# Two attention layers on one core: next input and left operands of layer 1 in pieces of 8 KB a partition

## The chip, the cores and the metric

The kernel runs on one core of a Trainium2 chip. The core has a matrix engine (TensorE, PE in the profile; its weight loads are PEld), a vector engine (DVE), a scalar engine (ACT), a general one (GpSimd, POOL) and SyncE (SP), which issues most of the DMAs here. The DMAs of all queues run on 16 DMA engines. The metric is the device time of one execution in microseconds (us); smaller is better.

## The reference, cut to what matters

The input is x of shape (8, 512, 32, 32), float32: eight batches of 512 channels by 1024 tokens. Two layers follow one another, each with a residual and a group norm ahead of it:

```
x = x + L0(gn(x))        # qkv projection, 8-head attention, output projection
x = x + L1(gn(x))        # below

q, k, v = w_q @ x, w_k @ x, w_v @ x                    # 512x512 each, 8 heads of 64
attn = einsum('bhdq,bhdT->bhqT', q, k) * scale
attn = softmax(einsum('gh,bhqT->bgqT', w_head, attn))  # heads mixed before the softmax
attn = instance_norm(attn) * gamma + beta
out  = einsum('bhqT,bhdT->bhqd', attn, v).reshape(b, t, c) @ w_proj.T + b_proj
```

## The kernel before, in words

Layer 0 runs for all eight batches, then layer 1 for all eight. Between them the result of layer 0 lies in DRAM: `x1_d[b]`, 512 x 1024 float32, one row a channel (L503). Layer 0 writes it in eight tiles of 128 x 512 a batch (L1080). Layer 1 reads it twice: as the input `y` (L1270 for batch 0, `y_piece`, L1372, for the others) and again for the residual (L1564, `xs`, and L1620, `xs_last`, for the last batch).

The projections with `w_k`, `w_q` and `w_proj` are done by a Strassen-like scheme with seven products. Its left operands are seven combinations of blocks of the weights, fields 0 to 6 of 2 KB a partition each. Layer 0 makes them once (L792) and keeps them in DRAM as `left_d`, one row of 14 KB a partition; layer 1 loads them again for each batch. `Projection.products` (L1406) says which field a product uses, and `ORDER` (L1396) in which order the products come.

**The steps of layer 1.** Attention of a batch b goes in steps p = 0 to 8, each of four parts t = 0 to 3 (`Attention1.step`, L1930). In a step p from 2 to 7:

- PE computes the scores of 128 queries: eight tiles `scores(p, 0..7)` (L1701), which ACT copies out of PSUM to `raw` (L1713). `raw` has two buffers: one for tiles 0 to 3, the first half (kh = 0), one for tiles 4 to 7, the second half (kh = 1).
- SP then regroups `raw` by DMAs from SBUF to SBUF: `regroup` (L1719), per half eight DMAs of 256 KB, s = 0 to 3 with two each, so 16 in a step. They are issued for the first half in parts 1 and 2, for the second half at the end of the step. They put the heads of one query group on the partitions, for the mixing of heads.
- `mix(p - 1, s)` (L1738) mixes the heads of the step before on PE; it needs the regrouped quarter s of both halves. `mix(p - 1, 0)` comes 4.75 us after the first scores of step p when nothing is late: three scores tiles and half a `values` (L1796) lie before it. `mix` takes two PSUM tiles out of three, the ones that the scores tiles leave when ACT has copied them.
- ACT takes the exponentials (L1751), DVE transposes them (L1766) and takes their statistics (L1780), PE multiplies with v (L1796).
- In odd steps (3, 5, 7) the sums of two steps are turned into reciprocals: `totals` (L1828) has three more small matmuls, four small DMAs by POOL to DRAM (`zd`, L1844), and then two DMAs of 256 KB by POOL that broadcast them to all partitions (`rzb`, L1856). These two belong to the next step in the order of the code, but POOL gets to them when the `zd` have landed: in steps 3 and 5 of every batch, and in step 7 of the last one, within the same step.

**The pieces.** While batch b is in its steps, the data of batch b + 1 are loaded in pieces, one a step, issued by SP in part t = 0 of steps 2 to 7 (`piece`, L2008, from the list `a.pieces`, L2049): four pieces of `y` (a chunk of 128 channels each, 512 KB, 4 KB a partition), then fields 0-1 and fields 4-5 of `left_k` (512 KB each). Fields 2-3 and field 6 follow in step 8. SP takes its instructions in the order of the code: in step p a piece stands behind the second half of the regroups of step p - 1 and ahead of the first half of step p. In the last batch there is no next one: the pieces are four chunks of `w_proj` of 256 KB, in steps 2 to 5 (L2072), and steps 6 and 7 have none.

SP's DMAs share eight semaphores in turn; a DMA waits until the one eight places before it has landed.

What follows the steps (from the first scores of step 7 to the first scores of the next batch) takes 127.6 us in every batch; it holds the other projections, `out1`, and the loads of `left_p`, `left_q` and `w_v`.

Of the kernel before, what the change touches and what calls it, by code (L numbers as in the profile page):

```python
# [9 lines left out]
F32 = mybir.dt.float32  # L10
# [8 lines left out]
P = 128  # L19
# [448 lines left out]
def tile_two_attention_layers(  # L468
# [19 lines left out]
    nc = tc.nc  # L488
# [11 lines left out]

    const = ctx.enter_context(tc.tile_pool(name="const", bufs=1))
    dram = ctx.enter_context(tc.tile_pool(name="dram", bufs=1, space=DRAM))
    x1_d = [dram.tile([C, T], F32, tag=f"x1_{b}", name=f"x1_{b}") for b in range(B)]  # L503


    def column(name, src):
# [206 lines left out]
    with ExitStack() as l0:  # L713
# [35 lines left out]
        }  # L749
        left_t = {}  # L750

        def left_tile(which, b):
            t = wpool.tile([P, 7, 2, HC], F32, tag="left", name=f"left_{which}_{b}")
            left_t[which] = t
            return t

        def load_left(which, b):
            t = left_tile(which, b)
            nc.sync.dma_start(out=t.rearrange("p f k o -> p (f k o)"), in_=left_d[which])

        a21 = {}

# [18 lines left out]
        def combine_left(which, parts=range(5)):  # L781
            t, a = left_t[which], a21[which]
            if 0 in parts:
                nc.vector.tensor_add(t[:, 3], a, t[:, 2])
            if 1 in parts:
                nc.vector.tensor_sub(t[:, 4], t[:, 3], t[:, 0])
            if 2 in parts:
                nc.vector.tensor_sub(t[:, 5], t[:, 0], a)
            if 3 in parts:
                nc.vector.tensor_sub(t[:, 6], t[:, 1], t[:, 4])  # L790
            if 4 in parts:
                nc.sync.dma_start(out=left_d[which], in_=t.rearrange("p f k o -> p (f k o)"))  # L792

        load_blocks("k")
        load_blocks("v")
# [266 lines left out]
        def out0(b):  # L1062
            def finish(i, j, x, y):
                if y is not None and isinstance(x, list):
                    for m in range(2):
                        nc.vector.tensor_add(y[:, m], y[:, m], x[m])
                    x = y
                elif y is not None:

                    into = x if j == 1 and i == 1 else y  # L1070
                    nc.vector.tensor_add(into, y, x)
                    x = into
                for m in range(2):
                    oc = 2 * i + m
                    dst = xs[b][oc][:, ts(j, FB)]
                    xm = x[m] if isinstance(x, list) else x[:, m]
                    nc.vector.scalar_tensor_tensor(
                        dst, xm, pb0[:, oc : oc + 1], dst, ALU.add, ALU.add
                    )
                    nc.sync.dma_start(out=x1_d[b][ts(oc, P), ts(j, FB)], in_=dst)  # L1080

            project0(f"pp0_{b}", "p", xa_t[b], finish)

# [158 lines left out]
        for b in range(B):  # L1242
            more = b + 1 < B
            ag = Agenda()
            ag.at(1, lambda: bias_xa(b))
            for c in range(NCC):
                ag.at(2 + 2 * c, lambda c=c: start_xa(b, c))
            for c, slot in enumerate((4, 7, 12, 15)):
                if b > 0:
                    ag.at(slot, lambda c=c: stats_out(b - 1, c))  # L1250
                if more:
                    ag.at(slot + 1, lambda c=c: load_x(b + 1, c))
            if b < 3:

                which = ("k1", "q1", "p1")[b]
                ag.at(1, lambda which=which: load_blocks(which, tag="junk"))
                for i, slot in enumerate((13, 14, 16, 17, 19)):
                    ag.at(slot, lambda which=which, i=i: combine_left(which, [i]))
            if more:
                stats0(b + 1, ag, 18)  # L1260
                for c in range(NCC):
                    ag.at(51 + 3 * c, lambda c=c: normalize0(b + 1, c))
                ag.at(32, lambda: load_left("k", b + 1))
                ag.at(33, lambda: load_left("v", b + 1))
            else:

                def load_first():
                    t = n_t["1"] = shared.tile([P, NCC, T], F32, tag="n", name="y_0")
                    for c in range(NCC):
                        nc.sync.dma_start(out=t[:, c], in_=x1_d[0][ts(c, P), :])  # L1270

                ag.at(20, load_first)
                for slot, fn in zip((22, 25, 28), group_stages(0, B - 1, small_psum)):
                    ag.at(slot, fn)
                ag.at(32, lambda: load_left("q1", 0))
                ag.at(33, lambda: load_left("k1", 0))
                for c in range(NCC):
                    ag.at(49 + 4 * c, lambda c=c: normalize_to(n_t["1"][:, c], 0, c))
            attention0(b, ag)
            slot = NI + 2  # L1280
            if more:
                combine_right(f"{b + 1}", n_t[b + 1])
                qk0(b + 1, "k")
            else:
                combine_right("y1", n_t["1"])
                first_q1()
            ag.flush()
            if more:
                load_left("q", b + 1)
                v0(b + 1)  # L1290
                load_left("p", b)
                qk0(b + 1, "q")
            else:
                load_left("p", b)
                first_k1()
                first_wv()
            combine_right(f"{b}_xa", xa_t[b])
            out0(b)
            tmp.clear()
# [6 lines left out]
    with ExitStack() as l1:  # L1306
# [58 lines left out]
        def p_piece(c):  # L1365

            if c == 0:
                left_tile(("p", B - 1))
                w_t["p", B - 1] = w_t["p", B - 1][:, :NCC]
            nc.sync.dma_start(out=w_t["p", B - 1][:, c], in_=w_projT[ts(c, P)])  # L1370

        def y_piece(b, c):  # L1372

            if c == 0:
                y_t[b] = shared.tile([P, NCC, T], F32, tag="n", name=f"y_{b}")
            nc.sync.dma_start(out=y_t[b][:, c], in_=x1_d[b][ts(c, P), :])

        def normalize1(b, c):
            normalize_to(y_t[b][:, c], b, c)
# [15 lines left out]
        class Projection:  # L1395
# [10 lines left out]
            def products(self, m):  # L1406
                w = w_t[self.key]
                left, right = {
                    1: (0, self.b11), 2: (1, self.b21), 3: (6, self.b22), 4: (2, self.t[:, 3]),
                    5: (3, self.t[:, 0]), 6: (4, self.t[:, 1]), 7: (5, self.t[:, 2]),  # L1410
                }[m]
                if m == 2:
                    self.ps[2] = self.ps.pop(1)
                else:
                    self.ps[m] = m_psum(f"{self.nm}_{m}")
                for i in range(2):
                    for k in range(2):
                        nc.tensor.matmul(
                            self.ps[m][:, i], w[:, left, k * HC + i * P : k * HC + i * P + P],
                            right[:, k], start=(k == 0 and m != 2), stop=(k == 1),  # L1420
                            skip_group_check=True,
                        )
# [135 lines left out]
        def out1(b, t):  # L1558
# [4 lines left out]
            for i, j in ((0, 0), (1, 1), (1, 0), (0, 1)):  # L1563
                nc.sync.dma_start(  # L1564
                    out=xs[i][:, :, ts(j, FB)],
                    in_=x1_d[b][i * 2 * P : (i + 1) * 2 * P, ts(j, FB)].rearrange(
                        "(m p) t -> p m t", p=P
                    ),
                )

            def begin(i, j, y):
# [21 lines left out]
        def out1_last(a):  # L1593
# [22 lines left out]
            def inputs():  # L1616

                x = rawpool.tile([P, NCC, T], F32, tag="raw", name="xs_last")
                for oc in range(NCC):
                    nc.sync.dma_start(out=x[:, oc], in_=x1_d[b][ts(oc, P), :])  # L1620
                wsum = epool.tile([P, 2 * T], F32, tag="e", name="wsum")[:, :C]
                nc.vector.tensor_add(wsum, w[:, 0], w[:, 1])
                for n in range(2, NCH):
                    nc.vector.tensor_add(wsum, wsum, w[:, n])
                kept.extend((x, wsum))
# [61 lines left out]
        class Attention1:  # L1687
# [242 lines left out]
            def step(self, p, t, ag):  # L1930
# [73 lines left out]
                        self.regroup(p, kh, s)  # L2004
                if t == 3 and p % 2 == 0 and p >= 4:
                    self.divide(p // 2 - 2, nc.gpsimd)
                if older and t == 0:
                    self.piece()  # L2008
                ag.run(4 * p + t)

# [22 lines left out]
        for b in range(B):  # L2033
# [12 lines left out]
                    ag.at(i, stages[i])  # L2046
                ag.at(3, v_sums)
            if more:
                a.pieces += [lambda c=c: y_piece(b + 1, c) for c in range(NCC)]  # L2049
                a.pieces += [lambda f=f: left_piece(("k", b + 1), f, 2) for f in (0, 4)]  # L2050
                ag.at(4 * NT, lambda: left_piece(("k", b + 1), 2, 2))
                ag.at(4 * NT, lambda: left_piece(("k", b + 1), 6, 1))
                for c in range(NCC):
                    ag.at(24 + c, lambda c=c: normalize1(b + 1, c))

# [13 lines left out]
                ag.at(4 * NT + 1.5, lambda: k_go(6))  # L2069
                ag.at(4 * NT + 2.5, lambda: k_go(7))  # L2070
            else:
                a.pieces += [lambda c=c: p_piece(c) for c in range(NCC)]  # L2072

                def prelude():
                    out_products.extend(out1_last(a))
# [108 lines left out]
```

## Time and profile before

| what | value |
|---|---|
| median of 3 runs | 3907.03 us (3902.49 to 3908.03) |
| profiled execution, its own time | 3899.99 us |
| its span, from the first to the last instruction | 3898.1 us |
| granted TensorE clock | 0.999 |
| DVE, ACT, POOL busy | 73%, 50%, 5% of the span |
| first scores of layer 1, batch 0, step 0 | at 1778.4 us |
| a batch of layer 1, from its step 0 to the next one's | 269.4 to 271.3 us (batches 1 to 6) |
| DMA issues on SP's queue | 1024 regroups, 28 `y` pieces, 28 pieces of `left_k`, others |

The page names, for each line of the kernel, the busy time of its group of instructions, and then the idle time of that engine just ahead of them and what ended it. Views of the waits, of the timeline and of chosen stretches of time (windows) go into a part of the span. Landings of single DMAs come from the trace's semaphore records: each DMA counts its semaphore up sixteen times, once for each DMA engine, and the last of these is its landing. Positions in a step are counted from its first scores matmul (L1701).

### The profile page before, as it was taken

What the parts mean: (1) busy time and instruction counts of PE and PEld (TensorE: products, weight loads), DVE (VectorE), ACT (ScalarE), POOL (GpSimd) and SP (SyncE); (2) the same over time, 40 slices, a digit from 0 to 9 for tenths busy, and PEclk for the clock granted to TensorE, in tenths of its full rate; (3) what the DMA queues carried; (4) which work ended last, traced back from release to release, by engine and by line L of the source; (5) the groups of instructions that cost most, each with busy time, mean ns of one, the idle gap of its engine ahead of it and who ended that gap; (6) DMA issues with size and microseconds to landing.
All of it is one profiled execution on the core that took longest, in us unless ns stands there. A gap on an engine that the chain in (4) does not pass through costs nothing. (4 is left out here: it accounts for less than half of the span.)

```text
span 3898.1 us, 95183 instructions
## 1 busy us (share of the span) xinstructions
PE 3845.0 (99%) x41612; PEld 1809.6 (46%) x41612; DVE 2840.8 (73%) x3921; ACT 1962.0 (50%) x2400; POOL 207.4 (5%) x210
## 2 busy tenths in 40 slices
PE   8999999999999999999999999999999999999999
PEld 4353535344353535344554544545545545445455
DVE  4858586675859485866967958859769668678598
ACT  1726354453627172534826717528438257176175
POOL 0000000000000000000110200201101102002000
PEclk9999999999999999999999999999999999999999
DMA  3313131111122121216947929749659479297385
GB/s 122 123 52 118 50 113 43 67 67 71 58 73 67 59 81 49 91 47 162 235 133 194 231 91 232 194 127 240 180 136 239 150 171 237 96 222 206 119 222 161
DMA packets 248440, 519.45 MB, mean 133 GB/s; under 512 B 49872, under 2 KB 57040, under 8 KB 241360
## 3 DMA queue, kind: packets, MB, share of 16 engines
q1 hardware_dynamic: 240832, 500.48, 45.3%
q0 software_dynamic: 7184, 12.81, 1.6%
q8 instruction: 328, 5.37, 0.6%
q14 instruction: 96, 0.79, 0.1%
HBM read 197.16 MB, written 46.92 MB: 63 GB/s over the span
## 5 line engine op out<-in xcount | busy, mean ns | idle before, releaser
L1766 DVE STREAM_TRANSPOSE et<-e 128x2048 f32<-128x2048 f32 x256 | 590.0, 2305 | 190.4 <-ACT e L1751 189.3
L1796 PEld LDWEIGHTS a<-et,v 128*64 128x64 f32 x16384 | 505.7, 138 | 283.8 <-issue 266.1
L1780 DVE BATCH_NORM_STATS2 bn<-e 128x6 f32<-128x512 f32 x1024 | 635.7, 683 | 0.0
L1107 ACT ACTIVATE e<-s 128x1024 f32<-128x1024 f32 x512 | 496.9, 1024 | 233.0 <-PE s L1102 233.0
L1713 ACT COPY raw<-s 128x1024 f32<-128x1024 f32 x480 | 470.1, 1018 | 224.8 <-PE s L1701 201.3
L1751 ACT ACTIVATE e<-m 128x1024 f32<-128x1024 f32 x512 | 496.2, 1021 | 165.7 <-issue 62.4
L1796 PE MATMUL a<-et,v 128*64 128x64 f32 x16384 | 553.3, 224 | 0.0
L1701 PE MATMUL s<-k,q 64*64 64x512 f32 x4096 | 513.2, 605 | 2.7 <-DVE v L1060 1.4
L1102 PE MATMUL s<-q,k 64*64 64x512 f32 x4096 | 490.4, 594 | 2.3 <-ACT e L1107 2.3
L1117 DVE TENSOR_TENSOR zacc<-zacc,e 128x1024 f32<-128x1024 f32 x384 | 467.5, 1217 | 27.2 <-ACT e L1107 1.4
L1130 PE MATMUL a<-e,v 64*64 64x512 f32 x4096 | 484.1, 589 | 0.0
L1738 PE MATMUL m<-re,wmix 32*32 32x512 f32 x8192 | 306.2, 599 | 14.8 <-DMA re<-raw 11.8
L1130 PEld LDWEIGHTS a<-e,v 64*64 64x64 f32 x4096 | 156.7, 133 | 282.8 <-issue 282.5
L1102 PEld LDWEIGHTS s<-q,k 64*64 64x64 f32 x4096 | 146.2, 133 | 284.4 <-issue 220.2
L1844 POOL DMA_DIRECT2D zd<-rz x96 | 52.5, 552 | 3361.9 <-DMA y<-x 1846.6
L1701 PEld LDWEIGHTS s<-k,q 64*64 64x64 f32 x4096 | 127.2, 132 | 216.0 <-issue 95.5
L1812 ACT COPY q<-a 64x256 f32<-64x256 f32 x256 | 94.0, 367 | 138.7 <-PE a L1796 137.1
L1738 PEld LDWEIGHTS m<-re,wmix 32*32 32x32 f32 x8192 | 68.1, 103 | 154.3 <-ACT raw L1713 65.9
L1509 PE MATMUL pv_t<-wv,y 128*128 128x512 f32 x256 | 120.6, 609 | 0.0
L920 PE MATMUL pv_p<-left_v,tmp 128*128 128x256 f32 x512 | 113.1, 379 | 0.0
L920 PE MATMUL pk_p<-tmp,left_k 128*128 128x512 f32 x256 | 112.5, 592 | 0.0
L920 PE MATMUL pq_p<-tmp,left_q 128*128 128x512 f32 x256 | 112.5, 592 | 0.0
(332 smaller groups left out, 3918.3 us busy)
## 6 DMA issues: line engine op xcount, KB each, us to landing
re<-raw SPq DMA_DIRECT2D x1024, 256.0 KB
left_q<-left_q SPq DMA_DIRECT2D x17, 1792.0 KB
left_p<-left_p SPq DMA_DIRECT2D x17, 1792.0 KB
left_k<-left_k SPq DMA_DIRECT2D x10, 1792.0 KB
x<-in_x_dram SPq DMA_DIRECT2D x32, 512.0 KB
rzb<-zd SPq DMA_DIRECT2D x128, 128.0 KB
x<-x SPq DMA_DIRECT2D x64, 256.0 KB
y<-x SPq DMA_DIRECT2D x32, 512.0 KB
```

The lines of the kernel that those rows point to most:

```text
L920: nc.tensor.matmul(out, st, mv, start=start, stop=(k == 1), skip_group_check=True)
L1102: nc.tensor.matmul(ps[c * D : c * D + D, m], k[r, hp, k0 : k0 + D], q[r, hp, ts(f, FB)], start=True, stop=True,)
L1107: nc.scalar.activation(e[i], ps, AF.Exp, scale=S0 * S0)
L1117: nc.vector.tensor_add(zacc[g], zacc[g], e[i])
L1130: nc.tensor.matmul(acc[g][a][m * D : m * D + D], v[rows, kc, ts(2 * hp + m, D)], e[i][rows, m], start=(kc == 0), stop=(kc == NG - 1),)
L1701: nc.tensor.matmul(ps[c * D : c * D + D, m], qo_t[b][r, p, hp, ts(c, D)], k_t[b][r, hp, ts(kh, FB)], start=True, stop=True,)
L1713: nc.scalar.copy(dst, ps)
L1738: nc.tensor.matmul(ps[a // 2][c * 32 : c * 32 + 32, a % 2].rearrange("p (r h k) -> p h r k", r=2, h=2), wmix[rows].rearrange("p g i -> p ( ...
L1751: nc.scalar.activation(e[:, :, 2 * h : 2 * h + 2].rearrange("p r a k -> p a r k"), ps[h].rearrange("p a (r k) -> p a r k", r=2), AF.Exp,)
L1766: nc.vector.transpose(self.et[p, u].rearrange("p kb (r st a) g q -> p st kb r (a g q)", r=2, st=2)[:, st], self.e[p, s].rearrange("p r a ( ...
L1780: nc.vector.bn_stats(self.bn[n][:, p % 2, s, a], e[:, :, a].rearrange("p r k -> p k r"))
L1796: nc.tensor.matmul(acc[two * D : two * D + D, s].rearrange("p (x q) -> p x q", q=4), v_t[b][:, kb, ts(g, D)], et[:, kb, :, g], start=(kb = ...
```

## The change

- `x1_d[b]` becomes 256 x 2048: row p of block i holds channel p of chunk 2i and then channel p of chunk 2i + 1, so that two chunks are 8 KB side by side for a partition. Layer 0's writes, the two loads of `y` and the residual's loads follow that layout.
- A `y` piece is two chunks: 1 MB, 8 KB a partition. There are two instead of four.
- In DRAM (for the three weights of layer 1) the fields lie in the order 0, 1, 4, 5, 2, 3, 6. The first piece of `left_k` is fields 0, 1, 4, 5 (1 MB, 8 KB a partition); the rest, fields 2, 3, 6 (768 KB), is one DMA in step 8. `products` has the new places of the fields.
- Layer 0 writes and reads these three left operands in four DMAs instead of one, since its own tiles keep the old order of fields.
- A piece is issued in steps 2, 4 and 6 alone, not in 2 to 7. The last batch loads two chunks of `w_proj` in step 2 and two in step 4.

```diff
-    x1_d = [dram.tile([C, T], F32, ...) for b in range(B)]
+    x1_d = [dram.tile([C // 2, 2 * T], F32, ...) for b in range(B)]
...
+        def left_parts(which):
+            if which in ("k1", "q1", "p1"):
+                return ((0, 0, 2), (4, 2, 2), (2, 4, 2), (6, 6, 1))
+            return ((0, 0, 7),)
+
+        def left_moves(which, t):
+            for f, g, n in left_parts(which):
+                yield (
+                    t[:, f : f + n].rearrange("p f k o -> p (f k o)"),
+                    left_d[which][:, 2 * g * HC : 2 * (g + n) * HC],
+                )
...
-            nc.sync.dma_start(out=t.rearrange("p f k o -> p (f k o)"), in_=left_d[which])
+            for dst, src in left_moves(which, t):
+                nc.sync.dma_start(out=dst, in_=src)
...
-                    nc.sync.dma_start(out=x1_d[b][ts(oc, P), ts(j, FB)], in_=dst)
+                    nc.sync.dma_start(out=x1_d[b][ts(i, P), ts(NFB * m + j, FB)], in_=dst)
...
-        def y_piece(b, c):
-            if c == 0:
+        def y_piece(b, i):
+            if i == 0:
                 y_t[b] = shared.tile([P, NCC, T], F32, tag="n", name=f"y_{b}")
-            nc.sync.dma_start(out=y_t[b][:, c], in_=x1_d[b][ts(c, P), :])
+            nc.sync.dma_start(
+                out=y_t[b][:, 2 * i : 2 * i + 2].rearrange("p m t -> p (m t)"),
+                in_=x1_d[b][ts(i, P), :],
+            )
...
-                    1: (0, self.b11), 2: (1, self.b21), 3: (6, self.b22), 4: (2, self.t[:, 3]),
-                    5: (3, self.t[:, 0]), 6: (4, self.t[:, 1]), 7: (5, self.t[:, 2]),
+                    1: (0, self.b11), 2: (1, self.b21), 3: (6, self.b22), 4: (4, self.t[:, 3]),
+                    5: (5, self.t[:, 0]), 6: (2, self.t[:, 1]), 7: (3, self.t[:, 2]),
...
-                if older and t == 0:
+                if t == 0 and p in (2, 4, 6):
                     self.piece()
...
-                a.pieces += [lambda c=c: y_piece(b + 1, c) for c in range(NCC)]
-                a.pieces += [lambda f=f: left_piece(("k", b + 1), f, 2) for f in (0, 4)]
-                ag.at(4 * NT, lambda: left_piece(("k", b + 1), 2, 2))
-                ag.at(4 * NT, lambda: left_piece(("k", b + 1), 6, 1))
+                a.pieces += [lambda c=c: y_piece(b + 1, c) for c in range(2)]
+                a.pieces.append(lambda: left_piece(("k", b + 1), 0, 4))
+                ag.at(4 * NT, lambda: left_piece(("k", b + 1), 4, 3))
...
-                a.pieces += [lambda c=c: p_piece(c) for c in range(NCC)]
+                a.pieces += [lambda i=i: (p_piece(2 * i), p_piece(2 * i + 1)) for i in range(2)]
```

The order of the instructions on PE, ACT, DVE and POOL is the same in both kernels; only SP's list of DMAs differs. It has 15 more in layer 0 (three stores and two loads of left operands in four parts each), 28 fewer in the steps of layer 1, and two fewer each for `y_0` and `xs_last`: 17 fewer in all.

More of the change, by code (lines that the diff above doesn't have):

```diff
@@ L502, in tile_two_attention_layers @@
     dram = ctx.enter_context(tc.tile_pool(name="dram", bufs=1, space=DRAM))
-    x1_d = [dram.tile([C, T], F32, tag=f"x1_{b}", name=f"x1_{b}") for b in range(B)]
+    x1_d = [dram.tile([C // 2, 2 * T], F32, tag=f"x1_{b}", name=f"x1_{b}") for b in range(B)]
     def column(name, src):
@@ L791, in combine_left @@
             if 4 in parts:
-                nc.sync.dma_start(out=left_d[which], in_=t.rearrange("p f k o -> p (f k o)"))
+                for src, dst in left_moves(which, t):
+                    nc.sync.dma_start(out=dst, in_=src)
         load_blocks("k")
@@ L1268, in load_first @@
                     t = n_t["1"] = shared.tile([P, NCC, T], F32, tag="n", name="y_0")
-                    for c in range(NCC):
-                        nc.sync.dma_start(out=t[:, c], in_=x1_d[0][ts(c, P), :])
+                    for i in range(2):
+                        nc.sync.dma_start(
+                            out=t[:, 2 * i : 2 * i + 2].rearrange("p m t -> p (m t)"),
+                            in_=x1_d[0][ts(i, P), :],
+                        )
                 ag.at(20, load_first)
@@ L1370, in p_piece @@
             nc.sync.dma_start(out=w_t["p", B - 1][:, c], in_=w_projT[ts(c, P)])
-        def y_piece(b, c):
-            if c == 0:
+        def y_piece(b, i):
+            if i == 0:
                 y_t[b] = shared.tile([P, NCC, T], F32, tag="n", name=f"y_{b}")
-            nc.sync.dma_start(out=y_t[b][:, c], in_=x1_d[b][ts(c, P), :])
+            nc.sync.dma_start(
+                out=y_t[b][:, 2 * i : 2 * i + 2].rearrange("p m t -> p (m t)"),
+                in_=x1_d[b][ts(i, P), :],
+            )
         def normalize1(b, c):
@@ L1565, in out1 @@
                     out=xs[i][:, :, ts(j, FB)],
-                    in_=x1_d[b][i * 2 * P : (i + 1) * 2 * P, ts(j, FB)].rearrange(
-                        "(m p) t -> p m t", p=P
-                    ),
+                    in_=x1_d[b][ts(i, P)].rearrange("p (m t) -> p m t", m=2)[:, :, ts(j, FB)],
                 )
@@ L1618, in inputs @@
                 x = rawpool.tile([P, NCC, T], F32, tag="raw", name="xs_last")
-                for oc in range(NCC):
-                    nc.sync.dma_start(out=x[:, oc], in_=x1_d[b][ts(oc, P), :])
+                for i in range(2):
+                    nc.sync.dma_start(
+                        out=x[:, 2 * i : 2 * i + 2].rearrange("p m t -> p (m t)"),
+                        in_=x1_d[b][ts(i, P), :],
+                    )
                 wsum = epool.tile([P, 2 * T], F32, tag="e", name="wsum")[:, :C]
```

## The prediction

> **What bounds the kernel now.** I read the busy shares first, then who makes TensorE wait, then the steps of layer 1 one by one, then the landings of single DMAs.
>
> ```profile
> PE 3845.0 (99%) x41612; PEld 1809.6 (46%) x41612; DVE 2840.8 (73%) x3921; ACT 1962.0 (50%) x2400; POOL 207.4 (5%) x210
> ...
> q1 hardware_dynamic: 240832, 500.48, 45.3%
> ```
>
> PE is busy for 99% of the span, and the change takes nothing from its list, so it can only win PE's idle time. The waits of PE say what there is in the steps:
>
> ```profile
> PE m L1738 <- DMA re<-raw: 11.8, 17, 1.8
> ```
>
> That is `mix`, waiting for regrouped heads: 17 times, 11.8 us in all. The windows over steps 2 to 6 of batch 1 and what follows (length; busy time of PE, PEld, DVE, ACT, POOL; clock; DMA share; GB/s) show where:
>
> ```profile
> 2092.90:2113.40 20.50, 20.50 (x452) 11.02 (x448) 19.07 (x22) 16.91 (x21) 0.00 (x0) 1.00 0.96 233
> 2113.40:2134.20 20.80, 20.80 (x458) 11.36 (x454) 19.25 (x24) 16.91 (x21) 3.25 (x6) 1.00 0.96 247
> 2134.20:2155.40 21.20, 20.60 (x452) 11.07 (x448) 18.69 (x21) 16.95 (x21) 2.36 (x1) 1.00 0.93 235
> 2155.40:2176.20 20.80, 20.80 (x458) 11.36 (x454) 19.23 (x24) 16.91 (x21) 3.25 (x6) 1.00 0.96 244
> 2176.20:2198.00 21.80, 20.93 (x452) 11.19 (x448) 19.38 (x22) 17.94 (x22) 2.35 (x1) 1.00 0.93 229
> 2198.00:2325.60 127.60, 127.18 (x1242) 64.06 (x1238) 87.12 (x119) 38.88 (x51) 15.10 (x11) 1.00 0.47 139
> ```
>
> Steps 2, 3 and 5 are full of PE work (step 2: 20.5 of 20.5 us; odd steps hold 0.3 us more matmuls). Steps 4 and 6 aren't. Measured by the first scores matmuls, step 2 takes 20.52 us in six of eight batches; over that, the eight steps 4 are 8.6 us too long together and the eight steps 6 are 7.9 us: 16.4 us (0.4%). All other steps 2, 3, 5 together hold about 1.5 us, and the last row is 127.6 us in every batch, full.
>
> Just ahead of `mix(p - 1, 0)` stands a gap in all 16 steps 4 and 6; it sums to 12.5 us, and each time the `mix` starts 0.14 us after the second regroup of s = 0, second half, has landed. So what is late is the **regrouping of the odd steps 3 and 5**. After the even steps with a 512 KB piece these landings come early: median 0.9 us to spare, though in six of 21 there is none, and 1.1 us of waits in all. POOL's and PE's timelines of batch 1, step 3:
>
> ```profile
> 2124.33 2.19 POOL L1844 DMA_DIRECT2D zd<-rz  x4 [151.89 <-DVE rz L1838]
> 2130.80 1.12 POOL L1856 DMA_DIRECT2D rzb<-zd  x2 [4.29 <-DMA re<-raw]
> ```
> ```profile
> 2139.65 1.15 PE L1738 MATMUL m<-re,wmix 32*32 32x512 f32 x32 [0.60 <-DMA re<-raw]
> ```
>
> Two things make an odd step heavier: the `rzb` broadcast (512 KB, the first half of it issued 15.6 to 18.3 us into the step, while the second half is issued from 19.8 on) and the piece, 512 KB in odd and even steps alike. The change takes away the piece alone.
>
> **Which of the two is it?** Batch 7 separates them: its pieces have 256 KB in steps 3 and 5, and step 7 has `rzb` (16.0 us in) and no piece at all. The regroup that `mix` needs lands 26.59, 25.81 and 26.02 us into these steps; in the 14 steps 3 and 5 with 512 KB the mean is 26.36. It is needed at 25.42 (20.81 + 4.75 - 0.14). Step 7 of batches 0 to 6 has a piece but no `rzb`, and there it lands at 25.17 on average. Without a piece it is thus still late, without `rzb` mostly not. The waits in batch 7's window say the same:
>
> ```profile
> PE m L1738 <- DMA re<-raw: 1.4, 2, 1.1
> ```
>
> 0.70 us a wait, against 0.79 (11.1 / 14) in the other batches. The reason is in the landings: the six regroups of a first half come 1.06 us apart on the first of the 16 engines to finish whether a piece is in front or not, and the last two are issued only at 15.8 us, when ACT has copied. A piece lands at 12.2 to 14 us, delays the first regroups by 1 to 1.5 us on the slowest engine, and by the sixth (19 to 20 us, batch 7 too) little of it is left.
>
> **The change, part by part** (against the profiled execution, 3899.99 us, which is 7 us below the median of the three runs, 3907.03; I scale at the end).
>
> 1. *No piece in steps 3 and 5.* Bounds: at best all 14 waits go (11.1 us); at worst nothing, since a full 512 KB may have left no trace by 19 us. I take batch 7's row, where half the piece is gone: 0.09 us a step, so 0.18 for all of it, times 14 = **-2.5 us**. Next in line is then `rzb`. It would come earlier (15.8 to 16.0 us in batch 7, mean 17.0 otherwise) and hold up the first half's last regroups more: batch 7's excess per step 4 or 6 is 1.00 us, against 1.03 in the others. So I count no further gain in those 16.4 us.
>
> 2. *1 MB instead of 512 KB in steps 2, 4, 6* (seven batches, 21 pieces). A 4 KB packet takes 0.210 us on average on SP's queue, a 14 KB one 0.535 (median). An 8 KB packet lies between 8/14 of the latter (0.31) and two of the former (0.42); 8 packets per engine then take 2.4 to 3.4 us, where it is 1.7 now: 0.8 to 1.7 more. I take 1.3, from the 4 KB row, which is the nearest. What hides it: between the last landing of the first half and the first of the second lie 2.0, 2.3 and 2.5 us (medians of steps 2, 4, 6), where back-to-back regroups lie about 1.0 apart, so 1.0 to 1.5 us are free, about what is added. If nothing were absorbed there, 1.3 us less what each of the 21 steps has to spare adds up to 12 us; if all were, 0. A gain is excluded, as nothing in these steps gets lighter. I take a tenth, for the few steps with no spare: **+1.2 us**.
>
> 3. *The first half lands later by up to 1.3 us in even steps.* Its buffer is what ACT's first copy of the next step waits for. That copy starts at 1.16 us, and the first half lands at 0.36 and 0.08 us (medians after steps 2 and 4), so the copy could slip to about 1.8. Two copies (1.93 us) then end at 3.7, ahead of `mix` at 4.75: 0. Without that cover each 0.1 us beyond would cost 0.1 us in each of 14 steps.
>
> 4. *Order of data.* Each chunk of `y` and each field is issued no later than now (chunks 1 and 3 and fields 4-5 a step earlier). SP gets no new wait: a piece waits for the DMA eight places ahead, the first of the second half, which has landed by then. Step 7 loses its piece, but the 127.6 us behind it are full of PE work: 0.
>
> 5. *Layer 0*: 15 more DMA issues of 0.42 us (the median of L1270), 6.3 us of SP's time if nothing hid it; SP stands waiting for DVE and ACT there, and PE in layer 0 waits for no DMA of SP: 0. The same bytes move. The residual's loads keep packets of 2 KB.
>
> Sum: -2.5 + 1.2 = -1.3 us, 3898.7 for the profiled execution; in proportion, 3907.03 x 3898.7 / 3899.99 = **3905.7 us**.
>
> *Two rules against the rows.* Landings first: a piece lands 1.2 to 2.4 us after the regroup ahead of it, so its own start-up overlaps. The Trainium skill ("DMA: Bandwidth & Descriptors", section "Anatomy of one DMA") gives a fixed 2.0 us to each DMA; paid in full on 28 DMAs fewer it would make -56 us, which these landings contradict. And `rzb` is issued later where a piece was in the step (17.0 against 15.9). The same page ("Queues, rings and completion order") says that an engine changes between queues only at packet ends; longer packets would then hold POOL's small packets longer, some 4 x 0.16 us by the page, if they met. No piece is left in a step with `zd`, so the sum by it stays.
>
> **Rivals.**
> - *Faster: the piece is the last straw in odd steps.* For it: the odd step is the only one with 5.2 MB to move (4.2 of regroups), and 512 KB more is enough to turn 0.9 us to spare into a wait. Against it: batch 7. It would take 11.1 us off, less 1.2 of part 2: 3907.03 - 9.9 = 3897.1.
> - *Slower: the even steps get the wait.* 1 MB in front of the first half, then a second half that is not yet clear at 19.5 us: `mix(p - 1, 0)` in steps 3, 5, 7 waits. It decides once more than 0.9 us of the piece's delay lives on to the second half. Price 12 us, less 2.5 of part 1: 3907.03 + 9.5 = 3916.5. Against it: those 1.0 to 1.5 us free, and odd steps recover from a piece by the sixth regroup.
> - *It doesn't do what it says*: 8 KB packets move as two of 4 KB. Then part 2 costs its upper bound, 1.7 us of delay in place of 1.3; with 1.0 to 1.5 absorbed and 0.9 to spare this stays inside the forecast.
>
> **How the numbers follow.** Forecast 0.68, faster rival 0.18, slower rival 0.14. A measurement of this kernel can tell about 0.2% (7.8 us) from no change. The faster rival lies at -9.9 and passes that mark mostly (0.15 of its 0.18), the slower at +9.5 likewise (0.11 of 0.14); the forecast's own spread, -8 to +6, reaches a mark rarely (0.04 and 0.02): faster 0.19, same 0.68, slower 0.13. Range for 8 in 10: from the faster rival's 3897 to 3913, between the forecast and the slower rival.
>
> **What would show it.** Right: gaps ahead of `mix(p - 1, 0)` in steps 4 and 6 remain, around 0.6 us, with `rzb` issued near 16 us; steps 3, 5, 7 keep 20.5 to 20.8 us. Wrong to the good: steps 4 and 6 at 20.5. Wrong to the bad: step 3 at 21 us or more, with a wait for `re<-raw`. Packets of 8192 bytes on SP's queue taking 0.3 to 0.42 us would bear out part 2.

## The result, and the profile after

After takes 3914.98 us (median of 19 runs, 3906.57 to 3924.51), before 3905.13 (median of 19 runs, 3900.2 to 3913.31). The ratio is 1.0024, with a 95% interval of 1.0016 to 1.0031: about 9 us slower, where 1.3 us faster was forecast. The profiled execution of after takes 3910.06 us; its span is 10.2 us longer than that of before (3908.3 to 3898.1), 1.2 us of it ahead of layer 1 (first scores at 1779.6 us in place of 1778.4).

The page of after, PE's share, the queues, and the group of `values`; the last column of a group is the engine's idle time just before it, and what ended it. Below it stand the rows of q8 and of `values` from the page of before:

```profile
PE 3850.6 (99%) x41612; PEld 1811.8 (46%) x41612; DVE 2841.3 (73%) x3921; ACT 1962.1 (50%) x2400; POOL 207.6 (5%) x210
...
q1 hardware_dynamic: 238384, 500.48, 45.0%
q0 software_dynamic: 7184, 12.81, 1.6%
q8 instruction: 329, 5.39, 0.6%
...
L1817 PE MATMUL a<-et,v 128*64 128x64 f32 x16384 | 555.7, 224 | 1.9 <-issue 1.9
```
```profile
q8 instruction: 328, 5.37, 0.6%
...
L1796 PE MATMUL a<-et,v 128*64 128x64 f32 x16384 | 553.3, 224 | 0.0
```

The `values` had no idle time ahead of them in before (0.0); now they have 1.9 us, and no engine or DMA is named for it. PE's waits in after (total us, times, longest):

```profile
PE m L1759 <- DMA re<-raw: 13.6, 18, 2.5
...
PE a L1817 <- issue: 1.9, 6, 0.4
PE m L1759 <- issue: 1.4, 2, 0.8
```

The wait for regrouped heads, which the change was to shorten, is 1.8 us longer than before (11.8). The two lines with "issue" are new in their size: `values` had none in before, `mix` 0.3 us, once. The windows of batch 1, steps 2 to 6 and what follows, in the columns of the prediction:

```profile
2094.50:2116.60 22.10, 21.51 (x451) 11.10 (x450) 19.10 (x22) 16.89 (x21) 0.00 (x0) 1.00 0.97 240
2116.60:2137.70 21.10, 20.85 (x457) 11.39 (x454) 19.16 (x24) 16.89 (x21) 3.23 (x6) 1.00 0.87 219
2137.70:2158.90 21.20, 20.63 (x455) 11.09 (x451) 18.70 (x21) 16.96 (x21) 2.35 (x1) 1.00 0.98 259
2158.90:2180.00 21.10, 21.00 (x460) 11.52 (x458) 19.29 (x24) 16.96 (x21) 3.24 (x6) 1.00 0.88 216
2180.00:2201.20 21.20, 20.55 (x452) 11.03 (x450) 19.48 (x22) 17.87 (x22) 2.35 (x1) 1.00 0.98 262
2201.20:2328.80 127.60, 127.09 (x1242) 64.02 (x1240) 87.09 (x119) 38.84 (x51) 15.08 (x11) 1.00 0.46 135
```

Step 2, full in before (20.5 of 20.5 us), is 22.1 us long. Over the eight batches the steps 2 grow by 3.5 us together, 3 by 1.0, 4 by 0.7, 6 by 3.6; step 5 and the tail stay. So most of the loss is in steps with a piece. In step 2 none of it is ahead of the first `mix`; in step 6 1.3 us are. PE's timeline of that step 2, 12.8 us after its start (start, length, in brackets the idle time before):

```profile
2107.28 1.39 PE L1817 MATMUL a<-et,v 128*64 128x64 f32 x41
2108.60 1.09 PE L1759 MATMUL m<-re,wmix 32*32 32x512 f32 x16
2110.28 1.09 PE L1759 MATMUL m<-re,wmix 32*32 32x512 f32 x16 [0.59 <-issue]
2111.30 1.09 PE L1722 MATMUL s<-k,q 64*64 64x512 f32 x8
```

The 32 matmuls of one `mix` are cut in two by 0.59 us. Nothing in the program stands there: the same 32 go through in one stretch in before's timeline, at the same place in the step:

```profile
2107.03 1.14 PE L1738 MATMUL m<-re,wmix 32*32 32x512 f32 x32
```

**What PE lacks there is instructions.** Queue q8 brings them in packets of 16 KB (5.39 MB / 329). Numbering PE's instructions (matmuls, weight loads and a few others) from the program's start, PE stops in the middle of a group of identical matmuls of layer 1 at positions that are 193 or 194 modulo 256, eight of eight times after step 0 (longest 0.85 us): a packet is a block of 256. And it goes on 1.3 to 1.5 us after a packet of q8 has landed, every time. In the traces of the experiments below such stops stand at the same place in the block, and PE goes on 1.25 to 1.71 us after a landing. Packets and blocks match one to one if a packet is fetched about when PE enters the block ahead; no packet in any profile shown here is used sooner than 1.2 us after its landing. The same block in the two traces (us from the span's start):

```
         PE enters block   next packet moves    PE enters next block
before   2102.12           2103.83 to 2104.96   2107.12   2.16 after landing
after    2103.63           2107.70 to 2108.90   2110.28   1.38 after landing
```

A block that PE enters 6 to 18 us into a step lasts 6.0 us on average in before (4.8 to 7.1), so a packet stops PE when it lands later than some 4.6 us after PE has entered the block ahead (6.0 less the 1.4 from landing to PE's start; an estimate for the average block). The transfer itself takes 1.2 us in both; it starts 4.1 us after PE's entry into the block in place of 1.7, while the 1 MB piece and the regroups behind it are on the 16 engines (DMA share 0.97; it was 0.96 in before).

For what follows, two measures from each kernel's trace (one execution each). *Fetch landing*: mean time from PE's entry into a block to the landing of the next packet, for blocks entered 6 to 18 us into a step. *Block ends*: each interval between two starts of PE within three instructions of a block's end is compared with the same interval of the program elsewhere (the quickest quarter over all batches and kernels); excesses over 60 ns are added up over layer 1. By it the block ends cost 0.75 us in before and 7.0 in after: 6.2 of the 8.6 us by which the stretch from the first scores of batch 0 to those of step 7 of batch 7 grows. The two kernels with before's schedule of 512 KB pieces (layout_only, each_2k) have 1.4 and 3.3, which gives the scatter between executions.

### The profile page after: what moved, and what is told of

Same layout as the page of the kernel before. It is cut to its first block, busy times and chain, and to the rows that moved or that the text cites. A ratio compares the mean times of both kernels' runs of the same rounds, so it can differ in the third digit from the quotient of the medians.

```text
span 3908.3 us, 95174 instructions
## 1 busy us (share of the span) xinstructions
PE 3850.6 (99%) x41612; PEld 1811.8 (46%) x41612; DVE 2841.3 (73%) x3921; ACT 1962.1 (50%) x2400; POOL 207.6 (5%) x210
## 3 DMA queue, kind: packets, MB, share of 16 engines
q8 instruction: 329, 5.39, 0.6%
## 5 line engine op out<-in xcount | busy, mean ns | idle before, releaser
L1759 PE MATMUL m<-re,wmix 32*32 32x512 f32 x8192 | 308.3, 601 | 16.9 <-DMA re<-raw 13.6
```

Of the source, the lines that this page charges most:

```text
L1759: nc.tensor.matmul(ps[a // 2][c * 32 : c * 32 + 32, a % 2].rearrange("p (r h k) -> p h r k", r=2, h=2), wmix[rows].rearrange("p g i -> p ( ...
```

## The experiments

All ratios are to before, timed on the same chip in the same rounds, with 95% intervals. Landings are for steps 2, 4, 6 and for 3, 5, 7; the last two columns are delays ahead of `mix(p - 1, 0)`, counted like the block ends. All columns but the ratio are from one traced execution each, which can lie far from the median (rzb_sp: 3914.15 us, median 3923.89), so they don't add up to the ratio.

| kernel | ratio | fetch landing, us | block ends, us | mix, steps 4, 6 | mix, steps 3, 5, 7 |
|---|---|---|---|---|---|
| before | 1 | 2.75, 2.75 | 0.8 | 13.3 | 1.5 |
| after | 1.0024 (1.0016 to 1.0031) | 3.81, 2.47 | 7.0 | 14.5 | 1.8 |
| layout_only | 1.0002 (0.9994 to 1.0011) | 2.96, 2.67 | 1.4 | 14.9 | 1.2 |
| each_2k | 0.9998 (0.9989 to 1.0007) | 3.20, 2.70 | 3.3 | 16.4 | 0.7 |
| even_4k | 1.0018 (1.0010 to 1.0027) | 4.02, 2.50 | 7.1 | 14.0 | 1.4 |
| each_8k | 1.0044 (1.0027 to 1.0061) | 3.81, 3.31 | 14.0 | 18.4 | 1.2 |
| half_4k | 1.0051 (1.0035 to 1.0068) | 3.75, 3.22 | 7.7 | 24.5 | 1.0 |
| even_split | 1.0024 (1.0015 to 1.0033) | 3.21, 2.23 | 4.7 | 15.6 | 7.3 |
| three_4k | 1.0052 (1.0034 to 1.0070) | 3.98, 2.37 | 17.0 | 11.5 | 3.0 |
| rzb_sp | 1.0053 (1.0038 to 1.0069) | 4.00, 2.82 | 15.6 | 0.5 | 9.9 |
| rzb_split | 0.9974 (0.9965 to 0.9983) | 3.57, 3.04 | 8.3 | 0.0 | 0.9 |
| spread | 0.9956 (0.9942 to 0.9969) | 3.14, 2.66 | 0.6 | 1.4 | 1.5 |

**layout_only**: the new layout in DRAM and its four DMAs in layer 0, with before's pieces (from after).

```diff
...
-                if t == 0 and p in (2, 4, 6):
+                if older and t == 0:
...
-                a.pieces += [lambda c=c: y_piece(b + 1, c) for c in range(2)]
-                a.pieces.append(lambda: left_piece(("k", b + 1), 0, 4))
...
+                a.pieces += [lambda c=c: y_piece(b + 1, c) for c in range(NCC)]
+                a.pieces += [lambda f=f: left_piece(("k", b + 1), f, 2) for f in (0, 2)]
...
```

> Theory F (fetch): in the trace of after PE stands still nine times in the middle of a group of identical matmuls (3.5 us in all), always 1.4 us after a 16 KB packet of the instruction queue has landed and always at the same place in blocks of 256 PE instructions, so PE runs out of instructions while an 8 KB packet stream holds the fetch up. Rival C (clump): it is the 1 MB in one go, whatever its packets. Rival L (layout): the loss comes with the layout in DRAM (more DMAs in layer 0, two chunks side by side), not with the pieces. This kernel has the new layout and the old pieces (512 KB in 4 KB packets, one in each of steps 2 to 7). F and C: layer 0's +1.2 us and no stall inside a group: ratio 1.0003, within 0.9998 to 1.0008. L: about 1.0024, as after.

Ratio 1.0002, and no loss at block ends beyond the scatter, though PE stops twice inside a group (0.45 and 0.40 us), where no stop was expected. The layout is not the cause (L falls). Layer 1 begins at 1781.0 us here; in the kernels with the old layout it begins at 1778.4 to 1782.3, so the 1.2 us ahead of layer 1 are scatter.

**even_4k**: before with two pieces at a time in steps 2, 4, 6, so after's schedule in 4 KB packets.

```diff
-                if older and t == 0:
-                    self.piece()
+                if t == 0 and p in (2, 4, 6):
+                    self.piece(2)
```

> Old layout, two pieces of 512 KB back to back in steps 2, 4, 6 and none in 3, 5, 7: the schedule of after in 4 KB packets. F, if the length of a packet decides: no stall inside a group, ratio 0.9995 to 1.0005. C: the fetch is held up as in after, landing up to 5.7 us after PE has entered its block, some nine stalls, ratio 1.0015 to 1.0025. L: 1.0000.

1.0018, block ends 7.1 us, fetches landing as late as in after. The rival C holds, and F's packet length falls: at the same schedule 4 KB and 8 KB packets lose the same within what the runs can tell. The stops inside groups are three, not the nine or so expected, but longer (0.8 to 1.1 us). PE's waits in even_4k:

```profile
PE m L1738 <- DMA re<-raw: 14.6, 18, 1.6
...
PE a L1796 <- issue: 1.7, 2, 0.9
...
PE m L1738 <- issue: 1.1, 1, 1.1
```

**each_8k**: after with its 8 KB packets, but in pieces of 512 KB, 64 partitions at a time, one in each of steps 2 to 7; `left_k` likewise.

```diff
+            h = slice(64 * (c % 2), 64 * (c % 2) + 64)
             nc.sync.dma_start(
-                out=y_t[b][:, 2 * i : 2 * i + 2].rearrange("p m t -> p (m t)"),
-                in_=x1_d[b][ts(i, P), :],
+                out=y_t[b][h, 2 * i : 2 * i + 2].rearrange("p m t -> p (m t)"),
+                in_=x1_d[b][ts(i, P), :][h],
             )
...
```

> New layout, 8 KB packets, but 64 partitions at a time: 512 KB in each of steps 2 to 7 as in before. F, if the length of a packet decides: fetches late in steps 2 to 7, some five stalls inside groups, ratio 1.0012 to 1.0025. C: no such stall, 1.0003. L: 1.0024.

Worse than any forecast: 1.0044. On its face this speaks for F, against even_4k. But its 8 KB packets take 0.609 us on average in layer 1, those of after 0.407, so something else had changed with them.

**half_4k**: each_8k with two DMAs of 4 KB packets for each piece, still over 64 partitions.

```diff
-            nc.sync.dma_start(
-                out=y_t[b][h, 2 * i : 2 * i + 2].rearrange("p m t -> p (m t)"),
-                in_=x1_d[b][ts(i, P), :][h],
-            )
+            for m in range(2):
+                nc.sync.dma_start(out=y_t[b][h, 2 * i + m], in_=x1_d[b][ts(i, P), ts(m, T)][h])
...
```

> each_8k again (64 partitions, 512 KB in each of steps 2 to 7), with each piece as two DMAs of 4 KB packets. each_8k lost 14.0 us at the ends of PE's blocks and its 8 KB packets took 0.61 us on average, where those of after, over 128 partitions, took 0.41. If the half set of partitions makes the pieces slow, 4 KB packets take about 0.30 us in place of 0.21, the block ends lose 10 us or more and the ratio is 1.003 to 1.005. If it was the 8 KB packet: 0.21 us, block ends 1 to 3 us, ratio 0.9998 to 1.0008.

1.0051; its 4 KB packets take 0.312 us on average in layer 1 (0.225 in before). So it is the half set of partitions that makes these pieces slow, whether in one DMA (each_8k) or two, and each_8k says nothing for F. Where the time shows differs from what was expected: less at block ends (7.7 us, not 10), more ahead of `mix` (24.5). PE's waits in half_4k:

```profile
PE m L1772 <- DMA re<-raw: 22.1, 16, 3.0
...
PE a L1830 <- issue: 3.2, 7, 1.0
```

**each_2k**: before, with each piece as DMAs of 2 KB packets.

```diff
-            nc.sync.dma_start(out=y_t[b][:, c], in_=x1_d[b][ts(c, P), :])
+            for j in range(2):
+                nc.sync.dma_start(out=y_t[b][:, c, ts(j, FB)], in_=x1_d[b][ts(c, P), ts(j, FB)])
...
```

> Old layout and schedule, each piece cut into DMAs of 2 KB packets (y in halves of 256 KB; left by fields). F: the fetch has more room than in before (least room between landing and need 1.3 us there), but before has no stall to lose: 0.9990 to 1.0003; the waits ahead of the first mix of steps 4 and 6 stay. C: 1.0000. L: 1.0000.

0.9998: shorter packets win nothing either, and the fetches land no earlier (3.20 us).

**even_split**: two pieces in steps 2, 4, 6, the second at the end of t = 2.

```diff
-                if older and t == 0:
+                if t in (0, 2) and p in (2, 4, 6):
```

> Old layout; steps 2, 4, 6 take two pieces of 512 KB as in even_4k, but the second at the end of t = 2, behind the last regroup of the first half (some 10 us later). Clump theory in its strong form (the fetch of PE's instructions stands behind what is queued at once): fetches land as in before, 2.5 to 3.1 us after PE has entered its block, stalls at block ends under 3 us in all, ratio 0.9990 to 1.0008. Rival (bytes per step: 1 MB beside 4 MB of regroups is too much for the step, wherever it is put): as even_4k, 1.0012 to 1.0025, and the second half's regroups late, so that the first mix of steps 3, 5, 7 waits.

Neither forecast holds whole. The fetches land sooner than in even_4k (3.21 us in place of 4.02) and the block ends cost 4.7 in place of 7.1, 2.5 us of it in a single stop, but the ratio stays at 1.0024: the second piece now stands ahead of the second half's regroups, and the first `mix` of steps 3, 5, 7 waits 7.3 us where it was 1.4. The wait for regroups, in PE's waits of even_split, comes 27 times in place of 18:

```profile
PE m L1738 <- DMA re<-raw: 18.9, 27, 1.8
```

**three_4k**: before with three pieces at once in steps 2 and 4 (`piece(3)`).

> Old layout; three pieces (1.5 MB) back to back in steps 2 and 4, none elsewhere. From one piece to two the mean landing of a fetch went from 2.7 to 4.0 us behind PE's entry into its block, 6 to 18 us into the step. If it grows with what is queued at once it is about 5.3 us with three, where a block lasts 5.8 us and PE goes on 1.4 us after a landing: most blocks in that stretch then stall by about 1 us, two a step, 14 steps: 20 to 30 us, ratio 1.005 to 1.008. If the loss had another cause, in the regroups' landings: under 1.003, with the waits ahead of mix and not inside groups.

The dose counts (two runs): in steps 2 and 4 fetches land 4.69 us after the entry (one piece 2.78, two 4.08), block ends cost 17.0 us, the ratio is 1.0052. The ratio is at the low end of what was expected, landing and block ends are below it (5.3 us and 20 to 30 us). PE's waits in three_4k have "issue" at `mix`, at `values` and at the scores:

```profile
PE m L1738 <- issue: 2.7, 3, 1.4
...
PE a L1796 <- issue: 2.6, 5, 1.3
...
PE s L1701 <- issue: 1.4, 3, 0.8
```

**rzb_sp**: before, with the two DMAs of `rzb` on SP's queue at their place in the code.

```diff
-                self.zq.dma_start(
+                nc.sync.dma_start(
                     out=self.rzb[t * D : t * D + D],
```

> Before with rzb issued by SP at its place in the program, 0 to 5 us into steps 4, 6, 8, in place of POOL's queue, which issues it 15 to 18 us into the step ahead. If rzb alone makes the odd steps late, the waits ahead of the first mix of steps 4 and 6 (12.5 us) go almost wholly. The even steps then have a piece and rzb, 1 MB: by the clump theory the stalls at block ends grow to those of even_4k in steps 4 and 6 (some +5 us): ratio 0.9978 to 0.9992. If rzb is not the cause, the waits stay and the ratio is 1.001 or more.

The first half of the expectation holds: with `rzb` out of the odd steps and the pieces still in them, the waits of steps 4 and 6 fall from 13.3 to 0.5 us. So `rzb` makes odd steps late, with a piece beside it or without (after, even_4k); whether by its time or by POOL's queue isn't parted here. The second half was far too small: block ends cost 15.6 us, some 10 of it in steps 4 and 6, which have 1 MB, and 6 in steps 5 and 7; ahead of the first `mix` of steps 3, 5, 7 stand 9.9 us, nearly all in 5 and 7; and the ratio is 1.0053. PE's waits in rzb_sp:

```profile
PE a L1796 <- issue: 6.1, 7, 1.8
PE m L1738 <- ACT raw L1713: 5.2, 4, 2.0
PE m L1738 <- DMA re<-raw: 4.5, 8, 1.0
...
PE m L1738 <- issue: 1.9, 3, 0.7
```

**rzb_split**: rzb_sp, with the second half of `rzb` and the division at the next odd step.

```diff
+                    if p in (5, 7):
+                        self.broadcast(1)
...
-                    if p % 2 == 0 and p >= 4:
+                    if p == 8:
                         self.broadcast(1)
...
-                if t == 3 and p % 2 == 0 and p >= 4:
-                    self.divide(p // 2 - 2, nc.gpsimd)
+                if t == 3 and p in (5, 7, 8):
+                    self.divide((p - 4) // 2, nc.gpsimd)
```

> As rzb_sp, but the second half of rzb (256 KB) at the head of the next odd step, and the division by it in that step: each step has a piece and 256 KB of rzb. Waits ahead of mix in steps 4 and 6 go, fetches at 0.75 MB at once lie between one piece and two (about 3.3 us, stalls 2 to 4 us in all): ratio 0.9970 to 0.9985. If rzb is not the cause: 1.000 or more.

0.9974, as expected, and faster than before: the waits of steps 4 and 6 are gone. The block ends cost 8.3 us, twice what was expected, in steps 4 to 7, which have 768 KB at once.

**spread**: rzb_split, with each piece in two DMAs of 256 KB, one at t = 0 and one at the end of t = 2.

```diff
-                if older and t == 0:
+                if older and (t == 0 or t == 2 and self.b + 1 < B):
...
```

> rzb_split with each piece cut in two DMAs of 256 KB, one at t = 0 and one at the end of t = 2 of the same step. At t = 0 of steps 4 to 7 there are then 512 KB beside the regroups as in before (0.75 us lost at block ends), not 768 KB as in rzb_split (8.3 us). even_split's 512 KB at t = 2 cost 6 us ahead of the first mix of steps 3, 5, 7, about 0.28 us a step; half of that in 42 steps with room for some of it: 2 to 6 us. By the clump theory -7 + 2 to 6 against rzb_split: ratio to before 0.9960 to 0.9975. If the loss goes by bytes per step wherever they are: 0.9974 as rzb_split, or above.

0.9956: 17 us faster than before, a little better than the 0.9960 expected at best, and the block ends are back at 0.6 us; the first `mix` of steps 3, 5, 7 loses nothing against before (1.5 us). The same bytes cross the same queues in the same steps as in rzb_split. The intervals of the two ratios touch, but the slowest run of spread (3890.05 us) is quicker than the fastest of rzb_split (3891.93). The pieces' packets are 2 KB here; by themselves these won nothing (each_2k). Its waits and its windows of steps 2 to 6 of batch 1:

```profile
PE m L1740 <- DMA re<-raw: 2.6, 8, 0.6
...
PE a L1798 <- issue: 0.5, 1, 0.5
...
PE m L1740 <- issue: 0.2, 1, 0.2
```
```profile
2092.30:2112.90 20.60, 20.60 (x456) 11.07 (x452) 19.16 (x22) 17.01 (x21) 0.00 (x0) 1.00 0.96 231
2112.90:2133.70 20.80, 20.80 (x460) 11.35 (x458) 19.25 (x24) 16.91 (x21) 2.11 (x4) 1.00 0.92 229
2133.70:2154.60 20.90, 20.90 (x454) 11.13 (x452) 18.66 (x21) 16.91 (x21) 0.00 (x0) 1.00 1.01 242
2154.60:2175.40 20.80, 20.80 (x458) 11.35 (x457) 19.23 (x24) 16.91 (x21) 4.50 (x5) 1.00 0.96 243
2175.40:2195.90 20.50, 20.50 (x450) 11.01 (x448) 19.37 (x22) 17.89 (x22) 0.00 (x0) 1.00 1.02 246
```

All five steps are full of PE work, at a DMA share of 0.92 to 1.02: full engines do no harm by themselves here. By even_4k against three_4k, and rzb_split against spread, what does is a long stretch of work that is handed to them at once.

## Why the prediction was wrong, by its own steps

1. *No piece in steps 3 and 5, -2.5 us.* Nothing came: the delay ahead of the first `mix` of steps 4 and 6 is 13.3 us in before, 14.5 in after, 14.0 in even_4k. That batch 7 is late by `rzb` and not by its piece was read rightly, and rzb_sp shows it from the other side. The two figures taken from batch 7 were not borne out: neither its 0.09 us a step, nor its early `rzb`. In steps 3 and 5 of the other batches `rzb` is issued 16.9 us in on average in after, with no piece there, and 17.0 in before. So the faster rival, the piece as the last straw, falls too.

2. *1 MB in steps 2, 4, 6, +1.2 us.* **This is the step that failed.** The price of the transfer was right: 8 KB packets take 0.385 us (median; 0.407 on average), and 0.31 to 0.42 was estimated. What hides it was wrong, because only one reader of the DMA engines' time was asked, the regroups behind the piece. They do absorb it: the first `mix` of steps 3, 5, 7 waits 1.8 us in place of 1.5. The other reader is PE itself: its instructions stand on the page of before as the 328 packets of q8, at 0.6% of the engines' time, and the prediction has no term for them. Block ends cost 6.2 us more. The bound of 12 us holds the result, but for another reason than the one it was made from.

3. *ACT's first copy slips to about 1.8 us, at no cost.* After steps 2 and 4 it slips to 2.1 at most. PE waits for the copies for 0.3 us at the scores in both kernels, and once, in step 6 of batch 3, 1.2 us at `mix`, but that is after an odd step: right.

4. *Order of data, 0.* The tails sum to 893.4 us before and 893.2 after: right.

5. *Layer 0, 0.* layout_only is at 1.0002: right within its interval.

The slower rival gave 3916.5 us, close to the 3914.98 measured, and was yet wrong: its mechanism, the wait for regroups in steps 3, 5, 7, grew from 1.5 us to 1.8; that its number came near is luck. The mechanism exists, in even_split (7.3 us) and rzb_sp (9.9), where the extra bytes stand directly ahead of the second half. The sign "step 3 at 21 us or more" came true in batches 0, 1 and 6 (21.1 to 21.4 us), but the wait for `re<-raw` that was to go with it was 0.2 us in batch 1 and absent in the other two. Steps 2 and 6, which no sign named for the bad case, lost most.

Of the 8.6 us in layer 1, 6.2 are thus at block ends and 1.2 ahead of the first `mix` of steps 4 and 6, where executions scatter by more. The rest is in pieces under 0.5 us around the stops; its cause stays open.

The rule on queues that the prediction weighed, that long packets hold other queues, shows in no run: 8 KB against 4 KB (after and even_4k; over 64 partitions each_8k and half_4k) and 2 KB against 4 KB (each_2k, before) made no difference to the time that these runs can tell. The section cited for the fixed 2.0 us describes DMAs that GpSimd issues, while the 28 DMAs in question are SP's; no term of the sum uses it.

The Trainium skill ("Runtime: NRT & Kernel Launch", section "Instruction fetch mechanics") says that an engine's instructions come in blocks of 16 KiB, 256 of them, and that crossing a block is mostly hidden. The blocks are as this trace has them; hidden they are only while the next packet lands within some 4.6 us of the entry here; with later landings after lost 7.0 us at block ends and three_4k 17.0.

What holds the packet's start up: the packets queued on the engines, or the reads of the pieces and of `rzb` from DRAM, which regroups don't make? No run parts the two, but the trace of after shows that the reads aren't needed for it. In its steps 2, 4, 6 of batches 0 to 6, PE enters 42 blocks 6 to 18 us into the step. For 18 of them the last 8 KB packet of the piece has already ended, and until the fetch starts only the 2 KB packets of the regroups, 4-byte ones and two instruction packets of another queue are on the engines. Yet the next packet lands 3.88 us after the entry on average, against 3.97 for the 24 that PE enters while the piece still moves (before: 2.72 and 2.82). So regroups that stand behind a piece hold the fetch as well as the piece itself does. By what rule an engine takes up the packets that stand before it stays open. No run shows whether 8 KB packets over all partitions could be free if they came 512 KB at a time.

## What to carry to other kernels

Before merging transfers in a stretch where the DMA engines are full, ask who else uses them: a small transfer that PE needs at fixed intervals, such as its own instructions, decides over megabytes that have time to spare. An idle time marked "issue" inside a group of identical matmuls is the sign; compare its place with the packets of the instruction queue. Bytes that aren't urgent were cheapest here in small lots spread over the step (spread against rzb_split: the same bytes, 0.9956 in place of 0.9974, some 7 us), and moved away from the transfers with the least room (rzb_split: 0.9974).

## What was not expected of the hardware

PE's instructions are fetched only one block of 256 ahead in these traces, and PE goes on 1.25 to 1.71 us after the packet has landed when it stands waiting for it; a landing takes 2.75 us on average from the entry into the block beside one piece of 512 KB (before), 3.8 to 4.0 beside 1 MB (after, even_4k), 4.7 beside 1.5 MB (three_4k). And the DMAs over 64 partitions moved packets of the same length slower than those over 128: 0.312 us against 0.225 for 4 KB (half_4k, before), 0.609 against 0.407 for 8 KB (each_8k, after).
